# Attention with float32r products of 12-bit parts in place of Strassen sums, in a pre-norm attention and feed-forward kernel

## The chip, the core and the metric

The kernel runs on one core of a Trainium2 chip. The metric is device time in microseconds (us) of one execution, lower is better. The core has a matrix engine (TensorE, here PE, with PEld for its weight loads), a vector engine (DVE), a scalar engine (ACT), a general engine (POOL) and a queue engine that issues DMAs (SP). Each runs its own queue in order and waits on semaphores that the others raise. Matmul results land in PSUM, which has eight banks of 128 x 512 float32; DVE and ACT can read PSUM, POOL can't.

## The reference

One sequence of 1024 tokens, 512 channels; 32 heads of 128. Everything is float32.

```python
x = x + attention(layernorm(x))
x = x + ffn(layernorm(x))
# attention: q = n@wq[:, h, :128], k = n@wk, v = n@wv   (512 -> 128 per head)
#   s = q@k.T * 192**-0.5, causal;  p = softmax(s);  out = concat_h(p@v) @ wo
# ffn: three 512x512 layers whose weights are +1 or -1, relu between them, a scale per layer
```

## The kernel before

Tokens are cut into eight tiles of 128 rows (qt 0 to 7), heads into 16 pairs. A head has eight steps, one per query tile. The loop over `steps` (256 of them) issues in each step: the scores of the next step and their softmax, the transposed blocks of this step, and pieces of matrix products of other work, spread between by hand: `chain_of_pair` lists the query, key and value products of the next pair with costs and due steps, and `interleave` places them. `keep_in_program_order` pins matmuls, POOL sums, transposes and DMA issues to that order; other instructions are placed by the framework's scheduler.

Softmax (`probabilities`, `divide`): scores go to one PSUM tile `sc` of two banks; one DVE instruction (L694) adds the mask from SBUF, scales, and yields the row minimum; ACT takes the exponential and the sum (L705); DVE inverts the sum (L713), ACT multiplies (L714). DVE transposes 32 x 32 blocks into `tb` (L720), and 16 DMAs on SP (`exchange`, L66) put blocks in place as `pT`, for four query tiles at a time, twice per head. `attend` then multiplies values by `pT`; DVE copies the result (L801).

Products: queries and keys of a pair use two levels of Strassen's scheme (49 products for 64, `qk_products`), values one level (`v_products`, 7 for 8), output products one level (`o_products`). The weight and token sums that this needs are made on POOL (L79), kept in DRAM for the tokens (`t_kept`) and reloaded on ACT's DMA queue. The results are combined by ACT copies and DVE and POOL sums (L82, L79). All of these matmuls are float32. Only the feed-forward layers use float32r, a form in which PE makes one pass: each activation is split into a high part and a rest, and the weights are exact.

PSUM: `sc` one buffer of two banks, `st` three banks, `mm` three banks. A helper at L85 issues nearly all matmuls.

Of the kernel before, what the change touches and what calls it, by code (L numbers as in the profile page):

```python
# [1 line left out]

# [11 lines left out]
P = 128  # L14
# [13 lines left out]

@with_exitstack
def kernel(  # L30
# [20 lines left out]
    NQB = S // QB  # L51
    scale = DQ ** (-0.5)
# [9 lines left out]
    pinned, first_stage = [False], [True]  # L62

    def load(dst, src):

        tc.keep_in_program_order(nc.sync.dma_start(dst, src))  # L66

    def keep_first(ins):

        if first_stage[0]:  # L70
            tc.keep_in_program_order(ins)

    def keep_order(ins):

        if pinned[0]:
            tc.keep_in_program_order(ins)

    def pool_sum(*args):
        keep_order(nc.gpsimd.tensor_tensor(*args))  # L79

    def bank_sum(*args):
        keep_order(nc.vector.tensor_tensor(*args))  # L82

    def matmul(*args, **kw):
        keep_order(nc.tensor.matmul(*args, **kw))  # L85
# [5 lines left out]
    keep = pool("keep", 1)  # L91
    heads = pool("heads", 3)
    pairs = pool("pairs", 2)
    work = pool("work", 3)
    small = pool("small", 4)
    ps_sc = pool("ps_sc", 1, space=bass.MemoryType.PSUM)
    ps_st = pool("ps_st", 3, space=bass.MemoryType.PSUM)
    ps_mm = pool("ps_mm", 3, space=bass.MemoryType.PSUM)
    dram = pool("dram", 1, space=bass.MemoryType.DRAM)

    DH = D // 2

    wv_sb, wo_sb = {}, {}


    w_qk = const.tile([P, 7, 2, G, DN], F32, tag="wqk", name="w_qk")
    x_in = keep.tile([P, NT, D], F32, tag="pT1", name="x_in")

    def load_x(t):
        load(x_in[:, t, :], x_v[:, t, :])  # L110

    def load_qk_weights(which, g):
        blocks = w_qk[:, 2 * which : 2 * which + 2].rearrange("p j c h e -> p (j c) h e")
        for i in range(G):
            h = g * G + i
            if which == 0:
                src = wq_v[:, :, h, :DN]
            else:
                src = wkv_v[:, :, h * DN : (h + 1) * DN]
            load(blocks[:, :, i, :], src)  # L120

    def load_v_weights(g):
        wv_sb[g] = pairs.tile([P, NC, G * DV], F32, tag="wv", name=f"wv{g}", bufs=1)
        first = H * DN + g * G * DV
        load(wv_sb[g], wkv_v[:, :, first : first + G * DV])


    load_x(0)
    load_x(1)
    load_qk_weights(0, 0)  # L130
    load_qk_weights(1, 0)
    for t in range(2, NT):
        load_x(t)
        if t == TPB:
            load_v_weights(0)
# [5 lines left out]

    zeros = const.tile([P, P], F32, tag="p1", name="zeros")
    nc.vector.memset(zeros, 0.0)
    idle = ps_sc.tile([P, S], F32, tag="sc", name="ps_idle")
    for _ in range(10):
        nc.tensor.matmul(idle[:, :P], lhsT=zeros, rhs=zeros, start=True, stop=True)  # L146
# [5 lines left out]

    mask = const.tile([P, S], F32, tag="mask", name="mask")
    nc.gpsimd.memset(mask, 0.0)
    nc.gpsimd.affine_select(
        out=mask[:, S - P :],
        in_=mask[:, S - P :],
        compare_op=ALU.is_ge,
        fill=-BIG,
# [4 lines left out]

    tb = [
        keep.tile([P, NB, (qb + 1) * TPB, TPB, B32], F32, tag=f"tb{qb}", name=f"tb{qb}")
        for qb in range(NQB)
    ]  # L170

    def load_o_weights(g):
        tag = "wo" if g + 1 < NG else "wv"
        wo_sb[g] = pairs.tile([P, G, D], F32, tag=tag, name=f"wo{g}", bufs=1)
        load(wo_sb[g], wo_v[:, g * G : (g + 1) * G, :])
# [8 lines left out]
    def ffn_constants(part):  # L184
        if part:
            keep_order(nc.vector.tensor_scalar_mul(f_twice, f, 2.0))
            keep_order(nc.vector.tensor_scalar_mul(f_minus, f, -1.0))
            return
        for i, s in enumerate((s0, s1, s2)):
            load(s_sb[:, i : i + 1], s[None, :].to_broadcast((P, 1)))  # L190
        keep_order(nc.vector.tensor_scalar_mul(s_twice, s_sb[:, 0:2], 2.0))


        keep_order(nc.gpsimd.memset(f, 1.0))
        nc.gpsimd.affine_select(
            out=f,
            in_=f,
            compare_op=ALU.is_gt,
            fill=inh,
            base=n_exc - mixed * P,  # L200
            pattern=[[0, 1]],
            channel_multiplier=-1,
        )

    def sign_weights(i, k, slots):


        kt = const.tile([P, NC, D], k.dtype, tag=("p1", "u2", "u3")[i], name=f"k{i}")
# [11 lines left out]
    def mean_var(mv, xt, name):  # L220

        if len(xt.shape) == 2:
            stats = small.tile([P, 6], F32, tag="stats", name=f"stats_{name}")
            keep_first(nc.vector.bn_stats(stats, xt))
        else:
            stats = small.tile([P, 2, 6], F32, tag="stats2", name=f"stats_{name}")
            for half in range(2):
                nc.vector.bn_stats(stats[:, half, :], xt[:, half, :])
        keep_first(nc.vector.bn_aggr(mv, stats))

    def statistics(tiles, name):

        n = len(tiles)
        mv = small.tile([P, n, 2], F32, tag=f"mv{n}", name=f"mv_{name}")
        for t, xt in enumerate(tiles):
            mean_var(mv[:, t, :], xt, f"{name}{t}")
        std = small.tile([P, n, 1], F32, tag=f"std{n}", name=f"std_{name}")
        nc.scalar.activation(std, mv[:, :, 1:2], AF.Sqrt, bias=eps)
        rstd = small.tile([P, n, 1], F32, tag=f"rstd{n}", name=f"rstd_{name}")
        nc.vector.reciprocal(rstd, std)  # L240
        return [(mv[:, t, 0:1], rstd[:, t, :]) for t in range(n)]

    def normalise(xn, xt, mean_rstd):
        nc.vector.tensor_scalar(
            xn.rearrange("p (h d) -> p h d", h=2), xt, *mean_rstd, ALU.subtract, ALU.mult
        )

    def transposed(t, xn, name):
        pt = ps_mm.tile([P, NC, P], F32, tag="mm", name=f"ptx_{name}{t}")
        for c in range(NC):  # L250
            keep_order(nc.tensor.transpose(pt[:, c, :], xn[:, c * P : (c + 1) * P], ident))
        return pt

    xnT = const.tile([P, NC, S], F32, tag="xnT", name="xnT")


    mv_a = const.tile([P, NT, 2], F32, tag="mv_a", name="mv_a")
# [3 lines left out]
    def input_statistics(t):  # L261
        mean_var(mv_a[:, t, :], x_in[:, t, :], f"a{t}")
        keep_first(
            nc.scalar.activation(std_a[:, t, :], mv_a[:, t, 1:2], AF.Sqrt, bias=eps)
        )


    def input_rows(t):
        keep_first(nc.vector.reciprocal(rstd_a[:, t, :], std_a[:, t, :]))
        n = D if t else DH  # L270
        for first in range(0, D, n):
            rows = x_in[:, t, first : first + n]
            keep_first(
                nc.vector.tensor_scalar(
                    rows, rows, mv_a[:, t, 0:1], rstd_a[:, t, :], ALU.subtract, ALU.mult
                )
            )

    def input_columns(t):
        n = NC if t else NC // 2  # L280
        for first in range(0, NC, n):
            pt = ps_mm.tile([P, n, P], F32, tag="mm", name=f"ptx_a{t}_{first}")
            for c in range(n):
                keep_order(
                    nc.tensor.transpose(
                        pt[:, c, :], x_in[:, t, (first + c) * P : (first + c + 1) * P], ident
                    )
                )
            keep_first(nc.scalar.copy(xnT[:, first : first + n, t * P : (t + 1) * P], pt))
# [3 lines left out]
    def B(j, k):  # L293
        return xnT[:, 2 * j : 2 * j + 2, k * QB : (k + 1) * QB]

    t_new = const.tile([P, 3, 2, QB], F32, tag="T", name="T")

    T = [t_new[:, 0], t_new[:, 1], B(0, 1), t_new[:, 2]]

    def token_sums(which):  # L300
        terms = (
            (T[0], B(0, 1), B(0, 0)),
            (T[1], B(1, 1), T[0]),
            (T[3], B(1, 0), T[1]),
            (T[2], B(1, 1), B(0, 1)),
        )
        for n in which:
            pool_sum(*terms[n], ALU.subtract)

    def A_v(g, i, j):  # L310
        return wv_sb[g][:, 2 * j : 2 * j + 2, i * DV : (i + 1) * DV]

    def sums_of(a, tag, name, bufs):


        t = pairs.tile([P, 3] + list(a(0, 0).shape[1:]), F32, tag=tag, name=name, bufs=bufs)
        pool_sum(t[:, 0], a(1, 0), a(1, 1), ALU.add)
# [6 lines left out]

    def v_weight_sums(g):
        v_sum[g] = sums_of(lambda i, j: A_v(g, i, j), "wsum", f"wsumv{g}", 1)

    qk, vs, attn = {}, {}, {}

    def new_qk(h):  # L330
# [91 lines left out]

# [790 lines left out]
```

## Time and profile before

| | us |
|---|---|
| timed runs, median (lowest to highest) | 1316.43 (1316.06 to 1318.21) |
| profiled execution, first to last instruction (span) | 1313.3 |
| PE, share of the window 200 to 1200 us | 1000 of 1000 |
| 1240 to 1313.3 us (end of attention, feed-forward): PE busy | 68.7 of 73.3 |

The profiled execution has no time of its own beside its span. A page line names a source line, an engine, an operation and its tiles, the count, the busy time, the mean ns of one, and the idle time before it with what ended it. Recorded matmuls overlap, so their price is read from one start to the next. DVE does most of its work on scores (193 us at L694), block transposes (190 us at L720) and output sums (137 us at L657); ACT does 198 us of exponentials and 198 us of divisions; POOL's longest group is 86 us of query and key sums.

### The profile page before, as it was taken

How to read it: one execution, taken by the hardware profiler on the slowest of the kernel's cores; microseconds unless marked ns; L12 is line 12 of the kernel's file. 1: busy time of each engine (PE TensorE's matmuls, PEld its weight loads, DVE VectorE, ACT ScalarE, POOL GpSimd, SP SyncE). 2: the span in 40 equal slices, each digit the busy share in tenths (PEclk: the TensorE clock that was granted, in tenths of full speed). 3: DMA queues.
4: the chain of work that ended last, by engine and by line, in shares of the span. 5: the costliest groups of instructions: out<-in, count | busy, mean ns of one | idle time of the engine just before them, and what ended most of it. 6: DMA issues, size and time to landing. Idle time of an engine off the chain costs nothing.

```text
span 1313.3 us, 18986 instructions
## 1 busy us (share of the span) xinstructions
PE 1302.8 (99%) x6246; PEld 994.5 (76%) x6246; DVE 921.9 (70%) x1913; ACT 513.4 (39%) x959; POOL 628.2 (48%) x693
## 2 busy tenths in 40 slices
PE   9999999999999999999999999999999999999998
PEld 9867787777878777777877777787777777776667
DVE  5685867768686776867677686766768676776574
ACT  3543433433343343334334433434343343444331
POOL 2965462545446254544635454463555546342600
PEclk9999999999999999999999999999999999999999
DMA  5487675656767565676756567575657756554201
GB/s 193 135 233 165 164 175 139 164 129 158 182 158 178 135 169 123 164 179 159 179 135 165 127 165 180 158 178 135 163 129 167 179 158 175 138 141 111 54 1 64
DMA packets 137233, 197.12 MB, mean 150 GB/s; under 512 B 22320, under 2 KB 75312, under 8 KB 137136
## 3 DMA queue, kind: packets, MB, share of 16 engines
q1 hardware_dynamic: 103152, 141.89, 43.3%
q10 hardware_dynamic: 33984, 54.02, 16.4%
q8 instruction: 50, 0.82, 0.3%
q14 instruction: 47, 0.39, 0.1%
HBM read 92.54 MB, written 5.77 MB: 75 GB/s over the span
## 4 chain that ended last, share of the span: by engine, by line
PE 96%; DVE 1%; ACT 1%; DMA 0%; SPq 0%; POOL 0%; issue 0%; ACTq 0%; DVEq 0%; POOLq 0%
PE sc L85 18%; PE ps_av L85 18%; PE ps_o L85 14%; PE Y_qk L85 10%; PE Z_qk L85 7%; PE X_qk L85 7%; PE Y_v L85 7%; PE Z_v L85 4%; PE X_v L85 4%; PE ps_qk L85 2%; PE ps_h L85 2%; PE ps_out L85 1%; SPq L66 0%; POOL qk L79 0%; DMA t<-t_kept 0%; PE ps_idle L146 0%
## 5 line engine op out<-in xcount | busy, mean ns | idle before, releaser
L714 ACT ACTIVATE p<-p,rtotal 128x128 f32<-128x128 f32 (+7 forms) x256 | 198.4, 775 | 337.1 <-DVE rtotal L713 319.8
L705 ACT ACTIVATE p<-p,nmax 128x128 f32<-128x128 f32 (+7 forms) x256 | 198.1, 774 | 280.1 <-DVE nmax L694 262.8
L85 PE MATMUL sc<-qk 128*128 128x512 f32 (+3 forms) x768 | 290.4, 487 | 1.4 <-DVE nmax L694 1.4
L694 DVE CUSTOM_DVE_ANT_0 p<-sc,mask 128x128 f32<-128x128 f32 (+7 forms) x256 | 193.2, 755 | 96.6 <-PE sc L85 96.4
L85 PE MATMUL ps_av<-pT,v 128*128 128x512 f32 x744 | 253.7, 486 | 1.6 <-DMA pT<-tb 1.6
L85 PEld LDWEIGHTS ps_av<-pT,v 128*128 128x128 f32 x744 | 140.8, 190 | 115.7 <-issue 90.4
L85 PEld LDWEIGHTS sc<-qk 128*128 128x128 f32 x768 | 139.9, 190 | 76.4 <-issue 60.7
L720 DVE STREAM_TRANSPOSE tb<-p 128x128 f32<-128x128 f32 (+1 forms) x248 | 189.9, 770 | 4.5 <-ACT p L714 2.4
L79 POOL TENSOR_TENSOR qk<-qk 128x512 f32<-128x512 f32 x60 | 86.4, 1440 | 213.2 <-DVE rtotal L713 113.3
L657 DVE TENSOR_TENSOR acc<-acc,ps_o 128x512 f32<-128x512 f32 x204 | 136.9, 678 | 10.2 <-PE ps_o L85 8.5
L79 POOL TENSOR_TENSOR w_qk<-w_qk 128x512 f32<-128x512 f32 (+1 forms) x120 | 115.4, 967 | 2.4
L85 PE MATMUL Y_qk<-t,w_qk 128*128 128x256 f32 x412 | 108.6, 380 | 0.1
L82 DVE TENSOR_TENSOR u_qk<-Y_qk,p_qk 128x512 f32<-128x512 f32 (+1 forms) x120 | 74.1, 617 | 42.9 <-PE Y_qk L85 42.8
L79 POOL TENSOR_TENSOR u_qk<-u_qk,qk 128x512 f32<-128x512 f32 (+1 forms) x60 | 65.3, 1088 | 78.6 <-DVE u_qk L82 78.6
L85 PE MATMUL ps_o<-wo,attn 128*128 128x256 f32 (+1 forms) x392 | 102.4, 398 | 0.0
L801 DVE COPY attn<-ps_av 128x512 f32<-128x512 f32 x62 | 42.4, 684 | 71.1 <-PE ps_av L85 70.6
L82 DVE TENSOR_TENSOR qk<-Z_qk,u_qk 128x512 f32<-128x512 f32 (+1 forms) x120 | 73.8, 615 | 25.4 <-POOL u_qk L79 16.3
L85 PEld LDWEIGHTS ps_o<-wo,attn 128*128 128x128 f32 x392 | 72.9, 190 | 21.4 <-issue 7.9
L85 PEld LDWEIGHTS Y_qk<-t,w_qk 128*128 128x128 f32 x412 | 76.0, 190 | 17.0 <-issue 6.9
L79 POOL TENSOR_TENSOR attn<-attn,attn 128x512 f32<-128x512 f32 x15 | 19.1, 1274 | 145.0 <-DVE rtotal L713 145.0
L85 PE MATMUL X_qk<-xnT,w_qk 128*128 128x256 f32 x240 | 71.5, 380 | 0.0
L85 PEld LDWEIGHTS X_v<-wv,xnT 128*128 128x128 f32 x512 | 62.1, 192 | 1.8
(175 smaller groups left out, 2014.4 us busy)
## 6 DMA issues: line engine op xcount, KB each, us to landing
pT<-tb SPq DMA_DIRECT2D x496, 128.0 KB, 4.3
t<-t_kept ACTq DMA_DIRECT2D x176, 256.0 KB, 4.9
pT<-tb SPq DMA_DIRECT2D x496, 64.0 KB, 2.0
w_qk<-in_L_attn_wq_dram SPq DMA_DIRECT2D x32, 256.0 KB, 4.3
w_qk<-in_L_attn_wkv_dram SPq DMA_DIRECT2D x32, 256.0 KB, 6.7
wv<-in_L_attn_wkv_dram SPq DMA_DIRECT2D x16, 512.0 KB, 4.0
wo<-in_L_attn_wo_dram SPq DMA_DIRECT2D x16, 512.0 KB, 3.9
t<-t_kept ACTq DMA_DIRECT2D x60, 128.0 KB, 2.3
```

Source lines behind the costliest of these rows:

```text
L79: keep_order(nc.gpsimd.tensor_tensor(*args))
L82: keep_order(nc.vector.tensor_tensor(*args))
L85: keep_order(nc.tensor.matmul(*args, **kw))
L657: nc.vector.tensor_tensor(dst, dst, ps, ALU.add)
L694: nc.vector.tensor_tensor_reduce(out=p[:, :n], in0=sc[:, :n], in1=mask[:, S - n :], scale=-scale, scalar=BIG, op0=ALU.add, op1=ALU.min, ac ...
L705: nc.scalar.activation(p[:, :n], p[:, :n], AF.Exp, bias=nmax, scale=-1.0, accum_out=total)
L714: nc.scalar.activation(p[:, :n], p[:, :n], AF.Copy, scale=rtotal)
L720: nc.vector.transpose(tb[qb][:, :, : qt + 1, i, :].rearrange("p b c k -> p c b k"), p[:, :n].rearrange("p (c b k) -> p c b k", b=NB, k=B32),)
L801: nc.vector.tensor_copy(dst.rearrange("p (t a i) -> p a t i", a=NB, i=B32), ps)
```

## The change

Scores, queries, keys and values become three float32r products each, of parts that float32r holds exactly. A value a is split as hi + lo with hi of 12 bits; the product a b is (1 + 1/4096) hi hi' plus a middle product, minus 1/4096 of a third product of differences. The first two share one PSUM bank, the third has a bank of its own, and DVE joins the banks with a scaled sum. Strassen's scheme stays for the output products, which stay float32, as does attention times values.

```diff
+BASE = 4096.0
+UP = 1.0 - 0.5 / BASE
+    ps_two = pool("ps_two", 3, space=bass.MemoryType.PSUM)   # two banks each
+    ps_one = pool("ps_one", 2, space=bass.MemoryType.PSUM)
-    ps_sc = pool("ps_sc", 1, space=bass.MemoryType.PSUM)
-    ps_st = pool("ps_st", 3, space=bass.MemoryType.PSUM)
-    ps_mm = pool("ps_mm", 3, space=bass.MemoryType.PSUM)
+    def split_weights(what, h):                               # on POOL
...
+        pool_times(hi, r, UP)
+        pool_sum(big, r, plain(hi), ALU.subtract)
+        pool_times(big, plain(big), BASE)
+        pool_sum(diff, plain(hi), plain(big), ALU.subtract)
+    def qk_parts(what, h, k, ps, own=False):
...
+                times(t, ps[:, 0], 1.0 + 1.0 / BASE)          # ACT
+                plus_times(t, ps[:, 1], -1.0 / BASE, t)       # DVE
+            times(hi, t, UP)
+            pool_sum(lo, t, plain(hi), ALU.subtract)
+            plus_times(diff, plain(lo), -BASE, plain(hi))
...
+            pool_sum(big, plain(hi), plain(diff), ALU.subtract)   # keys: POOL comes last
+    def qk_unit(what, h, k):       # 8 matmuls into ps[:, 0], 4 into ps[:, 1], 512 wide
+    def v_unit(g, t):              # the same, 256 wide, one ps_one bank; ACT, then DVE
+    GROUPS = ((0, 4), (4, 2), (6, 2))                         # exchange in three parts
     def probabilities(h, qt):      # per half of up to 512 keys
+            for part in range(3):
+                matmul(ps[:, part // 2, :w], lhsT=q[:, part, :], rhs=k[:, part, :w], ...)
+                times(to[:, :rest], ps[:, 0, :rest], -(BASE + 1.0))
+                nc.vector.scalar_tensor_tensor(
+                    to[:, rest:], ps[:, 0, rest:w], -(BASE + 1.0), mask, ALU.mult, ALU.add)
             nc.vector.tensor_tensor_reduce(...)               # minimum, per half
+            nc.vector.tensor_tensor(nmin[0], nmin[0], nmin[1], ALU.min)
     def attend(h, grp, pT):
-            nc.vector.tensor_copy(...)
+        nc.scalar.copy(dst.rearrange("p (t a i) -> p a t i", a=NB, i=B32), ps)
+    # each step: weights of the next head (0: load, 1: split queries, 2: split keys; values
+    # of the next pair: load at 6 of the even head, split at 0 and 1 of the odd head)
+        if qt in (0, 1):
+            units.append((counted(qk_unit("qk"[qt], h, 1)), 4))
+        if qt in (4, 5) and h + 1 < H:
+            units.append((counted(qk_unit("qk"[qt - 4], h + 1, 0)), 4))
+        av = {2: (h - 1, 1), 3: (h - 1, 2), 6: (h, 0)}.get(qt)
...
+        if qt in (6, 7):           # one value tile in step 6, three in step 7
+    O_PARTS = {0: 2, 1: 1, 2: 2, 4: 1, 5: 1}                  # output products per step
```

The planner (`chain_of_pair`, `interleave`, due times), the token sums and their DRAM copies go; `spread` mixes the units of a step evenly, half of them before the division and half after. For the first four token tiles, the queries and keys of head 0 and the values of pair 0 are made in plain float32. The tail computes the first half of the tokens through the feed-forward layers first, where it was the second half.

## The prediction

> **What bounds the kernel now.** I read the page's busy line first, then what TensorE (PE) waits for, then single matmuls in the timeline.
>
> ```profile
> PE 1302.8 (99%) x6246; PEld 994.5 (76%) x6246; DVE 921.9 (70%) x1913; ACT 513.4 (39%) x959; POOL 628.2 (48%) x693
> PEclk9999999999999999999999999999999999999999
> ```
>
> ```profile
> PE ps_av L85 <- DMA pT<-tb: 1.6, 1, 1.6
> PE sc L85 <- DVE nmax L694: 1.4, 3, 0.6
> ```
>
> The second fence is the list of PE's waits (total, times, longest): its two largest are 1.6 and 1.4 us in a 1313.3 us span. PE is full, at full clock, and stalls only at the two ends. So a change is paid in PE work first, and then in any stall it brings.
>
> PE's price must be read from starts, since recorded matmuls overlap. Timeline (start, duration), then two rows of the chain that ended last, then the last layer's 256-wide matmuls:
>
> ```profile
> 609.11 1.02 PE L85 MATMUL sc<-qk 128*128 128x512 f32 x2
> 609.97 1.03 PE L85 MATMUL Z_qk<-t,asum 128*128 128x256 f32 x4
> ```
>
> ```profile
> 1277.69 9.49 PE ps_h L85 x40
> 1287.19 7.26 PE ps_out L85 x32
> ```
>
> ```profile
> 1308.37 1.60 PE L85 MATMUL ps_out<-w_signs_T,x 128*128 128x256 f32 x12
> ```
>
> A float32 matmul of 512 columns (two records) holds PE for 0.86 us, 1.68 ns a column. A float32r matmul of 512 holds it 7.26/32 = 0.227 us in the output layer and 9.49/40 = 0.237 in a hidden layer; of 256 columns (1.60 - 0.283, the last one's length)/11 = 0.120. Three float32r products of 512 cost 0.68-0.71 us: less than one float32 (0.86), but more than its 49/64 under two Strassen levels (0.66).
>
> **PE's work.** Before: 729,856 float32 columns x 1.681 ns = 1227 us, feed-forward 45, transposes and warm-up 15: 1287. After, counted in the built program: 271,360 float32 columns (attention times values, output products, first tile) = 456; queries and keys 1512 x 0.227 = 343; values 1488 of 256 columns x 0.120 = 179; scores 576 x 0.227 + 192 (384 wide) x 0.173 + 192 x 0.120 + 192 (128 wide) x 0.09 = 204; feed-forward 45, the rest 11: 1238. That is **-49 us**, or -28 if queries, keys and scores run at 0.237. I take 0.227, since there, as in the output layer, the stationary operand differs in every matmul; the hidden layers use each twice. Queries and keys gain nothing (344 before); the gain is in the scores (248 before).
>
> The Trainium skill, page "TensorE: Matmul & The Clock Gate", section "Back-to-back issue gap", gives N/2.4 + 2.5 ns for one warm matmul, 216 ns at 512 columns. No row here reaches it; by it the 2088 wide products would save another 23 us.
>
> **Can the other engines follow?** Rates come from these groups (mean ns before the bar's end) and tile rows (min/median/max):
>
> ```profile
> L555 ACT COPY p_qk<-X_qk 128x512 f32<-128x512 f32 x45 | 26.1, 580 | 52.9 <-PE X_qk L85 52.9
> L1146 DVE SCALAR_TENSOR_TENSOR osb<-ps_out,s_sb,acc 128x512 f32<-128x512 f32 x7 | 5.2, 750 | 5.9 <-PE ps_out L85 5.9
> L694 DVE CUSTOM_DVE_ANT_0 p<-sc,mask 128x512 f32<-128x512 f32 x32 | 22.1, 692 | 7.5 <-PE sc L85 7.5
> L79 POOL TENSOR_TENSOR w_qk<-w_qk 128x512 f32<-128x512 f32 x60 | 75.7, 1273 | 2.4
> ```
>
> ```profile
> L82 DVE TENSOR_TENSOR qk<-qk x60: 670/676/1555, 67.4 to 1156.7; 128x512 f32<-128x512 f32 x60
> ```
>
> ```profile
> L66 SPq DMA_DIRECT2D pT<-tb x992: 507/589/2335, 50.4 to 1217.7; - x199
> ```
>
> Per head, after. PE: eight steps of 4.1-5.0 us, 36.8. DVE: transposes 6.1, minima 7.7, masks 8 x 0.35 (from the 0.75 and 0.48 rows), query and key parts 8 x 0.75, value sums 4 x 0.48, product sums 7 x 0.68, small ones 1.7: 31. ACT: exp 7.7, division 6.2, scores out of PSUM 4.6, query and key parts 8 x 0.58, values 1.5, attention copies 1.3: 26. POOL: three weight splits of 2 x 0.6 + 2 x 1.27, four sums of 1.27, Strassen sums 4: 20. None exceeds PE's 36.8, so by throughput the change would win. But these queues run in order, the PSUM pools have two and three buffers, and each step now sends its data back and forth ACT-DVE-ACT-POOL-DVE. I therefore followed the queue order of one head with the durations above, 0.2 us from a matmul's end to its reader and 0.05 us per hand-over (the chain shows 0.02-0.05). PE's queue runs in order too, so whatever waits holds all matmuls behind it. Three places in the head stall it. Time 0 is PE's start of the head's step 0.
>
> *Step 2, output-product bank.* ps_one has two banks; attention holds one, so the second output product must wait for the sum of the first (acc) on DVE. Its queue: the query unit ends at 4.8; take-out 0.2 + 0.58; DVE correction 0.75; ACT high part 0.58; POOL low part 1.27; DVE difference 0.75; acc of an earlier product 0.68; reciprocal 0.15; ACT division 0.62; ACT key take-out 0.58; DVE correction 0.75, mask 0.35, minimum 0.69, key difference 0.75, transpose 0.57, then this acc 0.68. With hand-overs 10.25: ready at 15.05. PE's own work between (scores 0.52, key unit 2.72, product 0.86, scores 0.68, attention 0.86, product 0.86, attention 0.86) ends at 12.2. **Stall 2.9**, in the 30 heads that have output products: 87 us.
>
> *Step 5, key unit.* With two score tiles and one query tile the three ps_two buffers are full; the key unit needs the query unit's. From PE's start of step 4: ACT still divides and copies attention until 1.15; scores out 0.58, minimum 0.69, mask 0.35, minimum 0.42, combine 0.13, exp 1.04, then (DVE behind transpose 0.84 and acc 0.68) reciprocal 0.15, division 0.93, query take-out 0.58, correction 0.75: 7.45. PE is ready at 5.9: **1.55**, x 31 = 48.
>
> *Steps 6-7, value banks.* Value tile 1 needs the attention tile's bank, whose ACT copy stands behind this step's exp; that exp waits for two minima behind the key parts, which wait for the query difference from POOL. Carried on from 7.45 the copy ends at 18.35, PE is ready at 16.2: 2.15. Value tile 2 needs tile 0's sum, which on DVE stands behind the 1.24 us transpose, and this behind the 1.15 us division: 21.35 against 19.85: 1.5. **3.65**, x 31 = 113.
>
> *POOL and SP in odd heads.* SP needs 16 x 0.589 = 9.4 us to issue the last exchange (transpose done 3.4 before time 0); the next query weights are behind it: issued at 6.0, landed (4.3 us on the page) at 10.4. On POOL stand split 3.75, a value split 3.75, then the key sum 1.27: 19.4, against 17.25 when the second score tile wants it: 2.2 x 16 = 35.
>
> *Ends.* At the start POOL's four splits (15 us, from the first weights at about 8) and two sums precede the first scores, about 26 us; PE's 18 us of work there started at 6.4 (the first row of query products now): +2, and the tail's order, where values and feed-forward inputs are less overlapped, +6.
>
> Costed at nothing: the token-sum reloads that go (54 MB on ACT's queue; the two DMA queues use 60% of the DMA engines now); attention in 256-wide pieces (float32 is linear in columns: 0.43 against 0.86); the exchange in three parts, whose 48 issues a head x 0.589 = 28 us lie beside 37 us of PE, their results being due two to three steps later. Without that cover each late exchange would hold PE as the keys do.
>
> **Sum**, against the profiled span 1313.3, which lies 3.1 under the timed median 1316.43 (its own run is not timed apart): 1313.3 - 49 + 87 + 48 + 113 + 35 + 8 = 1555 in span, **1558 us** timed.
>
> **Rivals.**
> PE-bound, faster: the stalls vanish because results reach the waiting queues in time; 1316 - 49 + 8 = 1275 (1296 at 0.237). For it: every engine has slack per head. Against: PE gains only 1.3 us per head before costs, so a total stall above 1.3 us per head already decides for slower, and the step 5 hand-back alone (0.2 + 0.58 + 0.75 + hand-overs = 1.63 against 1.22 us of scores) leaves 0.4 with nothing else queued. 8%.
> Half hidden: take-outs and corrections shorter than their rows, or one detour off the chain; 283/2 = 141: 1416. 26%.
> Blocked further: DVE's 676 ns sum took up to 1555, mean 914, where POOL also worked; eight such two-input instructions per head (differences, combined minima) x 0.24 x 32 = 61: 1619. 10%. The Trainium skill, page "SBUF — State Buffer", section "Who interferes with whom", states this as a lock: the later of a DVE instruction with two SBUF inputs and a POOL instruction that reads SBUF waits for the other's end. It speaks against this change; by it an instruction could wait a whole 1.27 us.
> That float32r would not bring its rate: the feed-forward rows exclude it.
> The full stalls: 56%.
>
> **Numbers.** Forecast 1558. The range 1390 to 1640 takes in half hidden and blocked, and leaves out PE-bound and what lies beyond: about 0.15. Beyond 0.2%, about what a measurement of this kernel tells from no change: faster 0.07, within 0.01 (PE-bound's upper edge), slower 0.92.
>
> **What would show it.** After: PE's work in starts near 1240 us but PE's share of the span near 80%; in PE's waits, ps_o for DVE acc, ps_k for the query correction, ps_v for ACT's copy and DVE's value sum, sc for POOL, 1 to 3 us each, some 30 times. DVE near 1000 us, under 70%. Wrong would be: PE at 95% or more, or one engine above 90%; a float32r step far from 0.227; or stalls mainly elsewhere, such as on the exchange.

## The result, and the profile after

The changed kernel takes 1766.8 us (median of 4 runs, 1763.15 to 1769.33) against 1316.45: a ratio of 1.342, 95% interval 1.340 to 1.344. The forecast was 1558, with a range up to 1640: the direction was right, the size was not. The profiled execution has a span of 1767.6 us. Its page, busy times and clock, to be laid beside the first fence of the prediction:

```profile
PE 1395.2 (79%) x6588; PEld 1154.7 (65%) x6588; DVE 952.3 (54%) x2400; ACT 792.9 (45%) x1624; POOL 848.2 (48%) x667
...
PEclk8878989898998999999898989989898998989989
```

PE's share is near the 80% that was forecast and no engine is full. But the clock row is no longer all nines: the mean granted clock is 0.907, which makes 330 us at half rate (2 x 0.093 x 1767.6), where the profile of before has none inside its span. PE's waits (total, times, longest):

```profile
PE sc L77 <- POOL k L80: 138.1, 21, 10.6
PE ps_v L77 <- ACT attn L475: 50.0, 31, 2.7
PE ps_k L77 <- DVE t_q L86: 38.7, 31, 2.1
PE ps_o L77 <- DVE rtotal L423: 35.2, 15, 3.5
PE ps_o L77 <- DVE acc L536: 32.0, 18, 2.5
PE ps_v L77 <- DVE v L86: 21.2, 26, 1.0
PE ps_o L77 <- DMA wo<-in_L_attn_wo_dram: 16.2, 5, 11.6
PE ptx_a L264 <- DVE x_in L253: 11.4, 4, 5.2
```

The first six are the places named in the prediction, but the first of them, forecast as the smallest, is the largest. The whole list adds up to 368.5 us; before it was 7.2. One odd head's wait for the key sum, in the timeline of all engines (start, duration; in brackets the idle time before and what ended it):

```profile
726.98 1.49 POOL L83 TENSOR_SCALAR w_q<-raw_q 128x512 fp32r<-128x512 f32 x1 [3.46 <-DMA raw_q<-in_L_attn_wq_dram]
...
730.39 0.82 PE L77 MATMUL ps_av<-pT,v 128*128 128x256 f32 x4
...
732.73 1.49 POOL L83 TENSOR_SCALAR w_v<-raw_v 128x512 fp32r<-128x512 f32 x1
...
738.44 1.26 POOL L80 TENSOR_TENSOR k<-k 128x512 fp32r<-128x512 f32 x1
...
739.75 0.69 PE L77 MATMUL sc<-k,q 128*128 128x128 f32 x2 [7.79 <-POOL k L80]
740.24 2.02 PE L77 MATMUL ps_av<-pT,v 128*128 128x256 f32 x4
```

This head began at 715.04. PE is ready for the second score tile 16.9 us later (17.25 forecast); the key sum ends at 24.7 (19.4 forecast), behind a query split that starts at 11.9 when its weights have landed (10.4), and takes 5.75 us, and a value split of 5.71 (3.75 each). The two ps_av rows show the clock: the same four records take 0.82 us at full rate and 2.02 after the long wait. SP, ahead of those weights:

```profile
712.44 11.11 SPq L74 DMA_DIRECT2D pT<-tb  x16
723.65 0.53 SPq L74 DMA_DIRECT2D raw_q<-in_L_attn_wq_dram  x1
```

Sixteen issues take 11.2 us here, 10.1 us in half of the heads. From one start to the next it is 0.633 us, where 0.589, the duration alone, was reckoned; in this head one step took 1.73. The float32r rate, from PE's timeline at full clock:

```profile
746.00 2.02 PE L77 MATMUL ps_q<-x,w_q 128*128 128x512 f32 x8
747.85 1.03 PE L77 MATMUL ps_o<-wo,at 128*128 128x256 f32 x4
```

Eight products of 512 columns from start to start: 1.85/8 = 0.231 us, close to the 0.227 taken. With such rates for all shapes (0.119 at 256 columns, 0.109 at 128) PE's work fell by about 35 us, not 49 (an estimate).

### The profile page after: what moved, and what is told of

Read it like the earlier page. It is cut to its first block, busy times and chain, and to the rows that moved or that the text cites. A ratio compares the mean times of both kernels' runs of the same rounds, so it can differ in the third digit from the quotient of the medians.

```text
span 1767.6 us, 21131 instructions
## 1 busy us (share of the span) xinstructions
PE 1395.2 (79%) x6588; PEld 1154.7 (65%) x6588; DVE 952.3 (54%) x2400; ACT 792.9 (45%) x1624; POOL 848.2 (48%) x667
## 4 chain that ended last, share of the span: by engine, by line
PE 32%; DVE 16%; POOL 15%; SPq 15%; ACT 12%; DMA 5%; issue 5%; ACTq 0%; POOLq 0%; DVEq 0%
SPq L74 15%; PE ps_av L77 7%; PE ps_o L77 5%; PE ps_q L77 5%; PE ps_v L77 5%; PE sc L77 4%; POOL w_q L83 3%; PE ps_k L77 3%; ACT p L424 3%; DVE p L402 3%; DVE tb L438 3%; POOL w_q L80 3%; ACT p L415 3%; DMA raw_q<-in_L_attn_wq_dram 3%; POOL w_v L83 3%
## 5 line engine op out<-in xcount | busy, mean ns | idle before, releaser
L77 PE MATMUL sc<-k,q 128*128 128x512 f32 (+3 forms) x1152 | 272.9, 361 | 150.1 <-POOL k L80 138.1
L415 ACT ACTIVATE p<-p,nmin 128x128 f32<-128x128 f32 (+7 forms) x256 | 198.4, 775 | 410.4 <-DVE nmin L413 360.9
L77 PEld LDWEIGHTS sc<-k,q 128*128 128x128 f32 x1152 | 206.9, 199 | 189.7 <-POOL k L80 144.1
L77 PE MATMUL ps_av<-pT,v 128*128 128x256 f32 (+3 forms) x1152 | 317.9, 419 | 7.0 <-DMA pT<-tb 7.0
L77 PE MATMUL ps_v<-w_v,x 128*128 128x256 f32 x1488 | 246.3, 318 | 71.6 <-ACT attn L475 50.0
L402 DVE CUSTOM_DVE_ANT_0 p<-sc,p 128x512 f32<-128x512 f32 (+3 forms) x384 | 213.6, 556 | 155.7 <-ACT p L89 146.9
L77 PEld LDWEIGHTS ps_v<-w_v,x 128*128 128x128 f32 x1488 | 216.5, 214 | 93.9 <-ACT attn L475 54.3
L77 PE MATMUL ps_k<-x,w_k 128*128 128x512 f32 x756 | 214.2, 420 | 38.7 <-DVE t_q L86 38.7
L77 PE MATMUL ps_q<-x,w_q 128*128 128x512 f32 x756 | 220.7, 422 | 0.0
L438 DVE STREAM_TRANSPOSE tb<-p 128x128 f32<-128x128 f32 (+7 forms) x256 | 197.8, 773 | 34.6 <-ACT p L424 26.1
L77 PE MATMUL ps_o<-wo,attn 128*128 128x256 f32 (+1 forms) x392 | 115.4, 422 | 16.8 <-DMA wo<-in_L_attn_wo_dram 16.2
```

What stands on the lines that cost most here:

```text
L77: pinned(nc.tensor.matmul(*args, skip_group_check=True, **kw))
L402: nc.vector.tensor_tensor_reduce(out=to, in0=ps[:, 1, :w], in1=to, scale=scale / BASE, scalar=BIG, op0=ALU.add, op1=ALU.min, accum_out=nmi ...
L415: nc.scalar.activation(p[:, :n], p[:, :n], AF.Exp, bias=nmin[0], scale=-1.0, accum_out=total)
L438: nc.vector.transpose(tb[h, grp][:, :, : qt + 1, qt - first, :].rearrange("p b c k -> p c b k"), p[:, :n].rearrange("p (c b k) -> p c b k" ...
```

## The experiments

Times are of one execution each, but for the medians of before and after; the kernel before took 1315.9 to 1318.0 beside them. "Waits" is the sum of PE's list of waits, "rest" the span less this sum, so PE's own time, with what the clock adds.

| kernel | us | waits | rest | clock |
|---|---|---|---|---|
| before | 1316.4 | 7 | 1306 | 1.00 |
| after | 1766.8 | 369 | 1399 | 0.907 |
| e1 value split later | 1662.0 | 267 | 1393 | 0.933 |
| e2 loads at step 6 | 1800.8 | 374 | 1425 | 0.914 |
| e5 loads at step 7 | 1713.3 | 303 | 1408 | 0.913 |
| e3 two-operation scaling | 1703.6 | 315 | 1387 | 0.921 |
| e6 = e5 and e3 | 1606.2 | 250 | 1355 | 0.950 |
| b1 attention in its own pool | 1771.8 | 383 | 1387 | 0.907 |
| c1 = e1 and e3 | 1616.6 | 257 | 1357 | 0.952 |
| c2 = c1 and b1 | 1623.7 | 245 | 1377 | 0.933 |
| e4 long wait filled | 1763.9 | 281 | 1481 | 0.935 |
| f3 = c1, bank waits filled | 1612.5 | 181 | 1430 | 0.968 |
| d1 all splits behind the key sum | 1600.4 | 237 | 1362 | 0.951 |
| d2 = d1, banks spread | 1557.4 | 210 | 1346 | 0.958 |
| f1 = d2, room on POOL | 1441.3 | 131 | 1309 | 0.977 |
| f2 = f1, product before keys | 1448.1 | 131 | 1315 | 0.980 |

My theory after the result: POOL's order of work, and what it waits for, sets the odd heads, and the waits cost a second time through the clock. The rival: waits only move, so that no order helps. The texts of what was expected call them A and B, with their own conditions.

**POOL's order (e1).**

```diff
-        if s in (8, 9) and not last:
-            split_weights("v", (g + 1) * G + s - 8)
+        if s in (8, 11) and not last:
+            split_weights("v", (g + 1) * G + s // 11)
```

> The second value split of a pair is issued at step 3 of the odd head instead of step 1, so that on POOL it stands behind the key sum and the key split and no longer ahead of them. Theory A (POOL's order of work sets the wait of the second score tile in odd heads): in the trace of after that split takes 5.7 us just ahead of the key sum, and PE waits 7.8 us there; the wait falls to about 2 us in 15 odd heads, 85 us, and some of the half-clock time that follows a long wait comes back (3.4 us per head at most, 51): 1766.8 becomes 1630 to 1685. Theory B (the walk only moves the wait: whatever POOL does later is wanted just as early): the 5.7 us turn up again at the next wait on POOL, above all the query parts of step 4, and the time falls by less than 30. Theory C (the landing of the next query weights behind the exchange on SP sets it): the query split still starts 3.5 us after POOL is free, and the wait falls by no more than the value split, so 2 us per odd head stay.

1662.0: theory A. The wait for the key sum fell from 138.1 to 37.6 us, with no new one in its place (the key unit's grew by 5).

**SP's order (e2, e5).** In e2 the loads stood ahead of the value weights at step 6, in e5 behind them at step 7:

```diff
-        if qt == 0 and h + 1 < H:
-            load_weights("q", h + 1)
-            load_weights("k", h + 1)
+        if i == 0 or qt == 7 and h + 2 < H:
+            load_weights("q", h + 1 + qt // 7)
+            load_weights("k", h + 1 + qt // 7)
```

> The query and key weights of a head are loaded two steps earlier, at step 6 of the head before the one that splits them, so that on SP they stand ahead of the last exchange's 16 issues (11.1 us) and not behind them; one more raw-weight buffer. Theory A (SP's order delays the query split, and with it the key sum): POOL's 76.8 us of waits for raw query weights (27 times, 5.0 the longest) go, and the score wait in odd heads falls from 7.8 to about 4.3: 3.5 x 16 = 56 us, 50 to 90 with the clock that comes back, so 1680 to 1715. Theory B (POOL would be late anyway, since the second value split and not the landing decides): POOL's wait goes but PE's score wait stays within 1 us, 1750 to 1770.

1800.8: both theories missed. POOL's wait for query weights fell from 76.8 to 2.7 us and PE's for the key sum from 138.1 to 48.4, but the value weights came late. At an odd head that PE began at 725.7, SP and then POOL:

```profile
723.59 0.53 SPq L74 DMA_DIRECT2D raw_q<-in_L_attn_wq_dram  x1
724.76 1.01 SPq L74 DMA_DIRECT2D raw_v<-in_L_attn_wkv_dram  x2
729.72 1.49 POOL L83 TENSOR_SCALAR w_v<-raw_v 128x512 fp32r<-128x512 f32 x1 [11.84 <-DMA raw_v<-in_L_attn_wkv_dram]
```

The value weights stand behind the query and key weights on SP: they are issued 1.0 us before the head begins (3.8 in after), and the first value split starts 4.0 us into the head instead of 0.3. The query parts stand behind it, DVE's query difference waits for these, and the output sums behind that on DVE: PE's waits for acc rose from 32.0 to 75.7, and those for the output weights from 16.2 to 57.3.

> Query and key weights loaded at step 7 of the head before, ahead of the exchange's 16 issues and behind the value weights; four raw-weight buffers for three. In the trace of after POOL idles 3.5 us for the query weights between the query parts and the query split in odd heads. Theory A (landing and POOL's work stand one behind the other, so that each is paid): the wait of the second score tile falls from 7.8 to 4.0 to 4.6, 3.5 x 15 = 52 us, with the clock 1700 to 1725. Theory B (only POOL's work counts): less than 15 us. Theory C (the loads delay something else on SP or POOL, as with step 6): 1767 or more, with waits for output sums or value weights up.

1713.3: theory A in time. The odd heads' wait fell by some 6 us, to 1.1 to 2.3, but part of that only changed its place: the waits for output sums grew from 67 to 105 us.

**The scaling (e3, e6).**

```diff
-        pinned(nc.gpsimd.tensor_scalar(out_, in_, factor, None, ALU.mult))
+        pinned(nc.gpsimd.tensor_scalar(out_, in_, factor, 0.0, ALU.mult, ALU.add))
```

> POOL's scalings get a second operation, plus 0.0, so that they have the form of the feed-forward sign weights, which took 608 ns for 128x512 in the trace of before against 1.49 to 1.56 us for these. If the one-operation form is what costs, each falls to about 0.6, a split from 5.7 to 3.9, and the score wait in odd heads by 2 x 1.8: 1766.8 becomes 1690 to 1715. If it is the float32 input (the sign weights are 8-bit), the scaling stays at 1.4 to 1.6 us and the time within 10 us of 1766.8.

1703.6: it is the form. The tile rows (min/median/max), after and then e3:

```profile
L83 POOL TENSOR_SCALAR w_q<-raw_q x32: 1487/1489/1907, 4.4 to 1603.0; 128x512 fp32r<-128x512 f32 x32
```

```profile
L83 POOL TENSOR_SCALAR w_q<-raw_q x32: 617/620/952, 4.5 to 1540.1; 128x512 fp32r<-128x512 f32 x32
```

The same product of the same tile takes 0.62 us with a second operation that adds zero, and 1.49 without.

> The same with the two-operation scaling: POOL's splits at the price that the prediction had used, and no landing to wait for. Theory A: query parts, query split 3.85, value split 3.85, key sum 1.27 after 7.2 us of the head give 16.2, against 16.9 when PE wants it: the odd heads' wait goes but for a few tenths, 1766.8 - 125 and 15 to 40 of the clock: 1600 to 1645. If landing and scaling overlap, so that one hides the other, 1670 or more.

1606.2, theory A: landing and scaling stand one behind the other, and gave 53 and 63 us alone, 161 together. In steady odd heads 0.82 us of the wait is left. The other waits stayed (waits of PE in e6):

```profile
PE ps_v L77 <- ACT attn L475: 48.7, 30, 2.7
PE ps_o L77 <- DVE acc L536: 36.3, 15, 2.5
PE ps_o L77 <- DVE rtotal L423: 35.6, 15, 2.4
PE ps_k L77 <- DVE t_q L86: 32.7, 31, 1.6
```

> The later value split (1662.0 alone) together with the two-operation scaling (1703.6 alone). If both work on one wait, the key sum on POOL in odd heads, then what the later split leaves of it, 37.6 us in 25 waits, is all that the faster scaling can still take: 1662.0 becomes 1615 to 1640, and PE's wait on POOL for score tiles falls under 15 us. If they were two costs, their gains would add: 1766.8 - 104.8 - 63.2 = 1599 or less.

1616.6: one wait, two ways to it; but 35.0 us of it are left, not under 15: about 2 us in most odd heads, behind the query split whose weights land late, and the first pair's.

**The banks (b1, c2).** In `attend`:

```diff
-        ps = ps_one.tile([P, NB, size, B32], F32, tag="one", name=f"ps_av{h}_{grp}")
+        ps = ps_two.tile([P, NB, size, B32], F32, tag="two", name=f"ps_av{h}_{grp}")
```

> Only the PSUM pool of the attention tiles changes: from the two-bank pool, which they share with output products and value tiles, to the pool of three double buffers, which in steps 2, 3 and 6 has one free. Theory A (the waits for output-product and value banks are a matter of where attention sits): in the trace of after PE waits 32.0 + 35.2 us for output banks and 50.0 for value banks behind ACT's attention copy; nearly all of it goes. In odd heads POOL's late key sum takes the place of some 2 us per head, so 60 to 100 of the 117 us come back, and with the clock 1766.8 becomes 1650 to 1715. Theory B (the banks are free late whatever shares them, since acc and the value sums stand behind the query and key parts on DVE): those waits stay above 80 us, or the wait on POOL's key sum grows by as much from its 138: 1740 to 1775.

1771.8: theory B. Two waits of PE in b1:

```profile
PE sc L77 <- POOL k L80: 212.1, 31, 11.8
PE ps_v L77 <- DVE v L86: 64.6, 46, 2.5
```

The 117 us went from the list, and the key sum and the value sums took them all: while POOL sets the pace, most of the time gained on PE is waited for at POOL.

> The three together: later value split, two-operation scaling, attention tiles in the pool of double buffers. With POOL out of the way, the bank waits (117 us of 365 in the trace of after) are gained in full and some of the clock's 104: 1480 to 1540. The wait of key products for the query correction on DVE stays at 35 to 45 us in 31 heads and is the largest. If instead the banks only hide the next late result (query and key parts, value sums), 1580 or more.

1623.7: the second of the two, 1580 or more; it is even 7 us slower than c1. Waits of PE in c2:

```profile
PE ps_v L77 <- DVE v L86: 84.1, 31, 3.2
PE sc L77 <- POOL k L80: 79.4, 31, 6.5
```

In c1 these were 22.1 and 35.0. The sum of the waits fell by 12 us, but the rest rose by 19 with the clock at 0.933 against 0.952: two gaps per head at the value tiles became one of 2.0 to 3.2 us.

**The clock (e4, f3).** Useless matmuls in front of the wait, here e4's; f3 has 4 to 8 of them at the second value tile of step 7 and the second output product of step 2:

```diff
+            if h % 2 and qt == 4 and m == 1:
+                for _ in range(24):
+                    matmul(ps[:, 0, :P], lhsT=ident, rhs=ident, start=True, stop=True)
```

> Ahead of the second score tile of step 4 in each odd head, 24 more float32 matmuls of 128 columns (0.215 us each, 5.2 in all) go into that tile's own bank and are overwritten: work that nobody needs, put where PE idles 7.8 us. Theory A (a share of the loss is PE's clock, which in the trace of after drops to half in 49 stretches, 330 us, beside such gaps, 104 us of PE's time): the wait for POOL shrinks by what the filler takes, the wait's end does not move, and the half-clock stretch behind it goes: 3.4 us x 16, so 1766.8 becomes 1700 to 1745 with a mean granted clock above 0.93. Theory B (the clock follows something else, or the half-rate stretches lie in time that is lost anyway): clock and time stay, 1755 to 1785, or the filler itself runs late and costs up to 5.2 x 16 = 83.

> The filler of the bank waits again (into the kernel with the later value split and two-operation scaling, 1616.6), each one fitted to the wait that it fills: 4 or 8 matmuls at the second value tile, 7 or 8 at the second output product, 409 in all, 99 us by the 0.243 us each that nine of them took in the earlier try. Theory A (those gaps halve the clock): the waits fall by 85 to 100 us, no wait grows, the half-rate time falls from 157 us to under 95, and the time falls by what the clock gives back, 15 to 30 us: 1587 to 1602. Theory B (no cost of the clock that is not waited for anyway): 1612 to 1640.

1763.9 and 1612.5: both times are theory B's. In e4 the waits fell by 87 us, and by estimate 83 were added (24 x 16 x 0.215). Half-rate time fell from 330 to 232 us, but only 3 us came back, which is within the spread of after's own runs (6.2). Counted in the traces, PE was busy for 207 us at half rate in after and for 190 in e4: what went was mostly half rate in which PE waited. Of the 12 gaps of 2.2 to 4.4 us that the filler left, 11 were followed by a stretch at half rate. In f3 the waits fell by 77 and the half-rate time from 157 to 104 (PE busy in it: 120 and 72), while the rest rose by 73, for some 99 us of filler (409 x 0.243, an estimate): 4 us came back. An earlier filler of nine matmuls at every place (d4, 1621.4) overfilled the waits: they fell by 89, the rest rose by 94. So filling raises the clock as A says, but nearly nothing came of it in time: in f3 the filler is some 9 us longer than the bank waits that it took away, and PE waits longer for POOL's key sum (35.0 to 41.7) and the value sum (22.1 to 28.4).

**Room for all (d1, d2, f1).** First every split behind the key sum, with the two-operation scaling:

```diff
-        if qt == 1 and h + 1 < H:
+        if qt == 2 and h + 1 < H:
             split_weights("q", h + 1)
-        if qt == 2 and h + 1 < H:
+        if qt == 3 and h + 1 < H:
             split_weights("k", h + 1)
-        if s in (8, 9) and not last:
-            split_weights("v", (g + 1) * G + s - 8)
+        if s in (10, 11) and not last:
+            split_weights("v", (g + 1) * G + s - 10)
```

> Two-operation scaling, and all weight splits one step or more later on POOL: queries at step 2, keys at step 3, the next pair's values at steps 2 and 3 of the odd head, so that POOL has nothing but the first sums ahead of the key sum of step 1. Compared with the later value split and the two-operation scaling together (1616.6, PE waits 35.0 us for POOL's key sum, 16 times). Theory A (the split of the query weights, still ahead of the key sum there, makes the rest of that wait): it falls under 8 us: 1616.6 becomes 1575 to 1600. Theory B (the key sum is late by its own chain of take-out, correction, high part, difference): the wait stays above 25 us, and four splits in two steps delay the query parts of step 4: 1605 to 1640.

1600.4: the key sum's wait is 6.2 us, as A says; the time is 0.4 above A's range, since the waits for value banks and the key unit grew by 11.

```diff
+        own, tag = (ps_two, "two") if grp else (ps_one, "one")       # attention
+        own, tag = (ps_two, "two") if i % 2 else (ps_one, "one")     # value tiles
```

> The same with PSUM spread differently: attention tiles of steps 2 and 3, and every second value tile, go to the pool of double buffers; the attention tile of step 6 stays with the output products. In the trace of the later split with two-operation scaling, waits for output banks were 59.9 us and for value banks 72.0; moving all attention tiles alone traded them for 84 us of waits for the value sum. Theory A (with the value tiles divided between the pools, no bank is wanted before its reader is done): those waits fall under 20 us together, 1400 to 1480 with the clock that comes back. Theory B (each bank is freed late by the in-order queues of ACT and DVE, wherever it lies): 1540 or more, the waits under other names.

1557.4, theory B's time, though the old waits fell to 20 us, as A has it: others came in their place. The attention tile of step 6 now waits 46.7 us for an output product's sum, and the waits for the output weights grew from 16.7 to 44.0 us.

```diff
-        if s in (10, 11) and not last:
+        if s in (8, 11) and not last:
...
-        if s == 14:
+        if s == 10:
             load_o_weights(g)
```

> The kernel with splits behind the key sum, two-operation scaling and spread banks (1557.4), with three edits: the first value split of the odd head goes back to step 0, where POOL waits anyway, so three splits and not four stand ahead of the query parts of step 4; the output weights are loaded four steps earlier into a second buffer; one pool of small tiles has three buffers instead of four. Left there are 46.7 us of waits of the attention tile of step 6 for the output product's sum (14 times, 3.4 the longest) and 44.0 for the output weights (16 times). Theory A (the sum on DVE stands behind the query difference, which waits for POOL's splits; the weights are late since SP loads them behind the exchange): both go but for some 15 us at the ends, 1557 becomes 1465 to 1500. Theory B (the sum is late because of DVE's own order): 1520 or more.

1441.3, better than A: one split fewer stands ahead of the query parts and the output weights come earlier, into a second buffer (not shown above), and both waits go. The two edits were not tried apart. Between the first pair and the tail one gap over 1.8 us is left (1.82) and four half-rate stretches of 3.4 us, where d2 had 17 (page and waits of f1):

```profile
PE 1304.6 (91%) x6588; PEld 1093.1 (76%) x6588; DVE 942.3 (65%) x2400; ACT 773.3 (54%) x1624; POOL 677.2 (47%) x667
...
PEclk8889999999999999999999999999999999999799
```

```profile
PE ps_k L77 <- DVE t_q L86: 41.9, 30, 1.8
PE sc L77 <- POOL k L80: 14.1, 14, 1.7
```

325 us have come back by order of work, buffers and a form of instruction, with every matmul as in after. The rest, 1309 us, is no less than before's 1306; some 21 of it are the clock's by estimate, as PE was busy for 42 us at half rate.

> The one with room on POOL and for the output weights, and the output product of step 5 ahead of the key products (0.86 us of matmuls more before they want their buffer; their wait was 0.97 to 1.5 us, 37.0 in all, 30 times). Theory A (the wait is the time that PE arrives too early): it falls to 5 to 15 us, 25 to 35 us less than without the edit. Theory B (what follows the keys is late by as much, since the product's sum and the key take-out change places): within 10 us.

1448.1, theory B: the key unit's wait fell to 16.1 us, and the key sum's rose to 51.1. Two earlier tries at it, which also put ACT's query take-out ahead of the division (c3, 1638.2; d3, 1579.3), were 14 and 22 us slower than c2 and d2, which they were added to.

## Why the prediction was wrong

Term by term, in span, by the profile of after:

| term | forecast | measured |
|---|---|---|
| PE's work | -49 | -35 |
| step 2, output banks | 87 | 67 (32.0 + 35.2) |
| step 5, key unit | 48 | 39 |
| steps 6 and 7, value banks | 113 | 71 (50.0 + 21.2) |
| POOL and SP in odd heads | 35 | 118 (14 waits of 7.3 to 9.4, and one of 1.6 in an even head) |
| ends | 8 | 66 (other waits, 73, less before's 7) |
| clock | none | about 100 |
| not placed | none | 28 |

The last row makes the sum 1767.6. It is no idle time: the page's busy time leaves 372 us of PE idle, of which the list of waits has 368.5, so it lies in PE's busy time, and no run separates it. The clock is an estimate: matmuls in half-rate stretches, start to start, against the same shapes at full rate (95 to 104 by two ways of counting; half of the 207 us in which PE was busy at half rate is 104).

The step that failed is **"POOL and SP in odd heads"**: its mechanism, place and order were right, its sizes were not: 118 us for 35. The split was priced 2 x 0.6 + 2 x 1.27 = 3.75, with the 0.6 from the row of the sign weights, an instruction of two operations; these have one and take 1.49. Two splits stand ahead of the key sum: 4.0 us. SP's issue was priced by the median duration, 0.589, and took 0.633 from start to start, with a longer step in some heads; in the head above the weights were in place 1.5 us later. Together 5.5 us more there. That e6, which takes both away, gave back 161 of the 209 us between result and forecast (and e1 105, c1 150) shows it; it is more than the 118 of the wait, since the clock came back too (0.907 to 0.950).

The second failure is an omission, about 100 us by the table: 283 us of stalls were forecast, with no term for the clock. The Trainium skill, page "TensorE: Matmul & The Clock Gate", section "HAM oscillation — how this bites in real kernels", warns of gaps beyond about 3.4 us; the measurement goes further, see below. What it costs in time isn't settled by a run that changes the clock alone: the fillers moved it, but added work and moved waits as well. f1 against after, with the same matmuls, puts 91 us of difference in PE's own time (1399 to 1309).

The ends were mis-sized as well, 66 for 8: in the first pair the score tiles wait for POOL's first sums (8.0, 9.8 and 10.6 us; the last two come after POOL itself stood still for 19.5 us ahead of a sum into acc, for DMAs), input transposes wait 11.4, and PE waits 11.6 for the last output weights. The bank terms came out smaller than forecast (177 for 248 with the key unit). That PE, held up at the key sum, arrives later at these waits is not the reason: in e6 and d1 the key sum's wait is down to 25.4 and 6.2 us, and the five waits still add up to 174 each. Why they are smaller stays open. That waits depend on each other, of which the sum of stalls knew nothing, is seen in b1.

Of the rivals, "PE-bound, faster" is out: with 131 us of waits left, f1's rest is about before's whole PE time. Without any wait this kernel would gain little, by estimate: PE's 35 us less the 28 not placed, or 18 by f1 (1306 less 1309 - 21). "Half hidden" fits no better: the three bank and key terms kept 177 of 248, and POOL's grew. "Blocked further" is seen, but its part of the time was not tried. DVE's minimum of two 128x1 columns in SBUF (min/median/max, after):

```profile
L413 DVE TENSOR_TENSOR nmin<-nmin,nmin x128: 136/159/1242, 61.1 to 1668.9; 128x1 f32<-128x1 f32 x128
```

In e1's timeline one of them stands beside a POOL sum:

```profile
740.99 2.67 POOL L80 TENSOR_TENSOR at<-attn,at 128x512 f32<-128x512 f32 x2
741.05 1.24 DVE L413 TENSOR_TENSOR nmin<-nmin,nmin 128x1 f32<-128x1 f32 x1
```

It ends at 742.29, some 1.3 us after the first of POOL's two sums began, which is the length of one: the wait for a whole POOL instruction that the prediction took from the Trainium skill's page "SBUF — State Buffer". The 128 instructions of the first row have a mean of 0.39 us against a median of 0.16, so 30 us of DVE's time went there; how much of it PE waited for isn't known.

## What to carry to other kernels

Price an instruction from a row of its own form, operand types and number of operations included: one wrong POOL row was worth 63 us of the miss by itself. When a full engine is traded for in-order chains across four others, look first at what is issued ahead of the short result that the bound engine wants, since moving long work behind it cost next to nothing here and gave 105 us. And once the matrix engine stalls by microseconds, add a term for its clock.

## What the runs showed of the hardware

POOL's multiplication of 128x512 float32 into float32r took 1.49 us with one operation and 0.62 us with a second one that adds zero.

The traces fit a clock that is decided in fixed windows of 3.41 us: in each of them all half-rate stretches start on one grid of that step. In c1, between 150 and 1380 us, by PE's gaps and the clock's stretches in the trace, a window with more than 1.95 us of PE idle was always followed by one at half rate, and, starting from full rate, one with under 1.7 us never was (in f3 two with 1.5 and 1.65 us were, so the lower bound isn't sharp). So single waits of 1.9 to 2.2 us halve the clock when they fall into one window (20 stretches, 46 gaps over 1.8 us, from 250 to 1400 us), though no gap there was longer than 2.8 us. By this, waits of a microsecond that fall into different windows cost only themselves, and the same time in one window up to half a window more, if PE has work all through the next one; this is worked out, not tried.
